# A GRU and a mixture of experts on one core: the state's dimensions dealt out anew, and the first loads reordered

## The chip, the cores and the metric

The kernel runs on one core of a Trainium2 chip. The metric is the device time of one execution in microseconds (us); for the kernel before it is 1520.65 us, the median of five runs (1519.76 to 1525.86).

## The reference

Sequences `x` of shape [8, 256, 512] go through a GRU whose start state is `cond_2048` [8, 512]; its outputs go through a mixture of eight experts (two for each token) and a shared feed-forward part, and the result is added to `x`:

```python
def cell(h, x):
    gi = x @ W_ih + b_ih
    gh = h @ W_hh + b_hh
    i_r, i_z, i_n = jnp.split(gi, 3, axis=-1)
    h_r, h_z, h_n = jnp.split(gh, 3, axis=-1)
    r = jax.nn.sigmoid(i_r + h_r)
    z = jax.nn.sigmoid(i_z + h_z)
    n = jnp.tanh(i_n + r * h_n)
    h_new = (1.0 - z) * n + z * h
...
combine = jnp.sum(topk_w[..., None] * jax.nn.one_hot(topk_ids, E, dtype=x.dtype), axis=1)
gu = jnp.einsum('th,ehf->etf', x, w_gate_up)
act = _silu_and_mul(gu)
eo = jnp.einsum('eti,eih->eth', act, w_down)
routed = jnp.einsum('te,eth->th', combine, eo)
shared = _silu_and_mul(x @ w_sh_gate_up) @ w_sh_down
```

W_ih and W_hh are [512, 1536] in float32, 3.15 MB each.

## The kernel before

Time is cut into 16 blocks of 16 steps; a block of all 8 sequences is 128 rows. The state has 512 dimensions on 128 partitions in NQ = 4 slots. Before the change, slot q of partition 32j+i holds dimension 128j+32q+i. With that order a 128x128 tile in which partition 32j+b holds sequence b's dimensions 128j to 128j+127 becomes, by VectorE's transpose of 32x32 squares, the transposed state. Weights whose rows are state dimensions have to be loaded in the same order: `by_state` (L122) gives four loads for it, each to 32 partitions.

**The weights' places.** w_ih, w_hh and later the experts' weights share one tile `we`: w_ih has the place of experts 6 and 7, w_hh that of experts 4 and 5. Biases and a row of ones have small places in `we` too.

**The head.** In program order: x_0 on SyncE's and ScalarE's queues in turn (8 loads, L119), the two bias rows on ScalarE's (L137, L138), w_ih in 12 loads on SyncE's (L142), h0 in 4 on ScalarE's (L147), x_1 in 8 and w_hh in 12 on SyncE's (L119, L152). VectorE turns x_0 (L299), and with that x_2's 8 loads are issued on SyncE's queue. Then, for each of the three gates g (r, z, n), `project(0, g)` (L340) multiplies x_0 with w_ih: four pieces, one for each q, of four matmuls to the four column groups; `spread_bias` (L256) spreads the bias row over 128 partitions by a matmul with ones, and ScalarE copies it to `bias` (L260). `end` (L355) adds product and bias into `gi` on VectorE. After gate 1 the sums for r and z are stored to DRAM (gid_rz, L366), after gate 2 those for n (gid_n, L368), both from SyncE's queue. `load_seeds` (L378) reads them back on SyncE's queue, four steps at a time, in the layout of the gates' banks: seeds (r and z) and seeds_n. `turn_seeds` (L388) transposes those for n. Then x_1 is transposed and the first gate of block 1 is projected (the loop at L862), the gates' banks are filled with the seeds (`open_gate`, L397, a ScalarE copy at L403), and step 0 begins.

Products, bias spreads and most other matmul results of the head share three PSUM buffers (tag "mm").

**A step** (`step`, L413) is 48 matmuls at L419, for each gate r, n, z 16: state slot q as the stationary operand (8 columns), w_hh's 128 columns of group j as the moving operand, the sum on top of the seeds in the gate's bank. VectorE transposes the bank (L430), ScalarE and VectorE make the gates and the new state (L438 to L455), GpSimd copies it to `hc` (L458). float32 matmuls are recorded twice, so a step has 96 records at L419.

**What fills PE between steps.** A queue of pieces, written out by the loop at L866, with a cost for each: the projections of later blocks, and from block 2 on the shared part (L705, L310). Blocks 0 and 1 take pieces of 33 times 0.86 each. Routing (`choose` at L472, and so on) has its own steps. Weights for the shared part and the experts are issued one entry of `loads` at a time on GpSimd's queue (L165), those of experts 4 and 5 after the last step. Last come 39 tiles of 128 routed rows, gathered (L752), transposed (L766), multiplied with their expert's weights (L659, L785) and added to the output by an indirect DMA (L791).

Of the kernel before, what the change touches and what calls it, by code (L numbers as in the profile page):

```python
# [13 lines left out]
ALU = mybir.AluOpType  # L14
# [11 lines left out]
def kernel(  # L26
# [100 lines left out]
    load_x(0, (nc.sync, nc.scalar))  # L127
# [10 lines left out]
    nc.scalar.dma_start(bias_h, b_hh[0 : 2 * D].unsqueeze(0))  # L138
    for g in range(3):
        cols = slice(g * D, (g + 1) * D)  # L140
        for ps, src in by_state(w_ih[:, cols]):
            nc.sync.dma_start(wih[ps, :, cols], src)  # L142
    h = state.tile([P, NQ, 32], F32, name="h")
    nc.vector.memset(h, 0.0)
    h0v = h0.rearrange("b (j q i) -> b j q i", q=NQ, j=4)
    for j in range(4):
        nc.scalar.dma_start(h[32 * j : 32 * j + B], h0v[:, j])  # L147
    load_x(1)
    for g in (0, 2, 1):
        cols = slice(g * D, (g + 1) * D)  # L150
        for ps, src in by_state(w_hh[:, cols]):
            nc.sync.dma_start(whh[ps, :, cols], src)  # L152
# [16 lines left out]
    def load_shared():  # L169
        load(*((wg[ps, :, 0:E], src) for ps, src in by_state(w_gate)))  # L170
        up = w_sh_gate_up.rearrange("d (two c f) -> two c d f", two=2, f=IM)
        down = w_sh_down.rearrange("(c f p) n -> c p f n", p=P, f=NF)
        for c in range(NSH):
            for two_i in range(2):
                parts = [(wsu[c][ps, :, two_i, :], src) for ps, src in by_state(up[two_i, c])]
                load(*parts[:2])
                load(*parts[2:])
            for f in range(NF):
                load((wsd[c][:, f, :], down[c][:, f, :]))

    def load_expert(e):
        for q in range(NQ):
            load((we[:, e, q, :], w_gate_up[e, q * P : (q + 1) * P, :]))
        for f in range(NF):
            load((we[:, e, NQ + f, :], w_down[e, f * P : (f + 1) * P, :]))


    ident = const.tile([P, P], F32, name="ident")
    make_identity(nc, ident)
# [4 lines left out]
    for st in [*seeds, seeds_n, seed_hn, *states]:  # L194
        nc.vector.memset(st, 0.0)

# [55 lines left out]
    nc.vector.tensor_tensor(bias_row[:, 0 : 2 * D], bias_row[:, 0 : 2 * D], bias_h, ALU.add)  # L252
    one = we[0:1, 2, 0, 0:P]
    nc.vector.memset(one, 1.0)
# [7 lines left out]
    b_hn = b_hh[2 * D : G3].rearrange("(j m) -> j m", j=4)  # L262
    for j in range(4):
        nc.gpsimd.dma_start(seed_hn[32 * j : 32 * j + B], b_hn[j].partition_broadcast(B))
# [32 lines left out]
    def transpose_x(k):  # L297
        xT = two.tile([P, NG, NQ, 32], F32, tag="xrT", name=f"xT_{k}")
        nc.vector.transpose(  # L299
            xT.rearrange("p g q s -> p (g q s)"), x_tiles.pop(k).rearrange("p g m -> p (g m)")  # L300
        )
        xT_of[k] = xT
        if k + 2 < NB:
            load_x(k + 2)
# [35 lines left out]
    def project(k, g):  # L340
# [13 lines left out]

        def end():  # L355
            nc.vector.tensor_tensor(
                gi[:, :, g, :],
                box["ps"].rearrange("p (j m) -> p j m", j=4),
                bias[:, g * D : (g + 1) * D].rearrange("p (j m) -> p j m", j=4),
                ALU.add,  # L360
            )
            if g > 0:
                to = gi_dram[k][g % 2].rearrange("j b t n -> (b t) j n")
                projected.add((k, "rzn"[g]))
                if g == 1:
                    nc.sync.dma_start(to.rearrange("p j (a n) -> p j a n", a=2), gi[:, :, 0:2, :])  # L366
                else:
                    nc.sync.dma_start(to, gi[:, :, 2, :])  # L368
# [9 lines left out]
    def load_seeds(c, of="nz"):  # L378

        k, o = divmod(c * SC, TS)  # L380
        steps = slice(o, o + SC)
        for g in of:
            assert (k, g) in projected
            tile_, src = (seeds_n, gi_dram[k][0]) if g == "n" else (seeds[c % NS], gi_dram[k][1])
            for j in range(4):
                nc.sync.dma_start(tile_[32 * j : 32 * j + B], src[j, :, steps, :])
# [18 lines left out]
    whh_v = whh.rearrange("p q (a j m) -> p q a j m", a=3, j=4)  # L405
# [5 lines left out]
    def step(n):  # L411
# [3 lines left out]
        for g, bank in banks.items():  # L415
            a = "rzn".index(g)
            for q in range(NQ):
                for j in range(4):
                    nc.tensor.matmul(  # L419
                        bank[32 * j : 32 * j + B, 0:P],  # L420
                        hT[:, q, 0:B],
                        whh_v[:, q, a, j, :],
                        start=False,
                        stop=(q == NQ - 1),
                        skip_group_check=True,
                    )
# [413 lines left out]
    transpose_x(0)  # L840
    nc.vector.transpose(states[0].rearrange("p q b -> p (q b)"), h.rearrange("p q i -> p (q i)"))
    for g in range(3):
        pieces = project(0, g)
        for piece in pieces[:-1]:
            piece[1]()
        spread_bias(g)
        pieces[-1][1]()
        if g > 0:
            load_seeds(0, "nzn"[g])
    turn_seeds(0)  # L850
    load_seeds(1)
# [3 lines left out]
    projections.append((0, lambda: transpose_x(1)))  # L855
# [6 lines left out]
    for _ in range(1 + NQ):  # L862
        projections.popleft()[1]()
    for g in banks:
# [128 lines left out]
```

## Time and profile before

| | |
|---|---|
| median of five runs | 1520.65 us |
| the profiled execution | 1519.18 us, its span 1517.4 |
| granted TensorE clock over the span | 0.989 |
| PE busy | 1443.5 us (95%) |
| VectorE, ScalarE, GpSimd busy | 49%, 28%, 17% |
| first matmul of step 0 | 55.95 us |
| w_ih's last load lands | 21.12 us |
| w_hh's last load lands | 39.51 us |
| matmuls L419, records | 24,576 of 273 ns |

The profile is of one execution, from the span's start. A group's mean is the time of one instruction from start to end; matmuls overlap, so the busy time of a group is less than count times mean. In the chain of work that ended last each row is a start, a length and what ran, and a DMA's length is from its issue to its landing. A DMA share of 1 means that the 16 DMA engines are full. In the view of waits a row names who waited for whom, the sum, the number of waits and the longest.

### The profile page before, as it was taken

How to read it: one execution, taken by the hardware profiler on the slowest of the kernel's cores; microseconds unless marked ns; L12 is line 12 of the kernel's file. 1: busy time of each engine (PE TensorE's matmuls, PEld its weight loads, DVE VectorE, ACT ScalarE, POOL GpSimd, SP SyncE). 2: the span in 40 equal slices, each digit the busy share in tenths (PEclk: the TensorE clock that was granted, in tenths of full speed). 3: DMA queues.
4: the chain of work that ended last, by engine and by line, in shares of the span. 5: the costliest groups of instructions: out<-in, count | busy, mean ns of one | idle time of the engine just before them, and what ended most of it. 6: DMA issues, size and time to landing. Idle time of an engine off the chain costs nothing.

```text
span 1517.4 us, 75290 instructions
## 1 busy us (share of the span) xinstructions
PE 1443.5 (95%) x33154; PEld 1057.7 (70%) x33154; DVE 750.8 (49%) x2782; ACT 423.2 (28%) x1786; POOL 258.6 (17%) x505
## 2 busy tenths in 40 slices
PE   4699999999999999999999999999999999999996
PEld 1487777787778787877787777887787754444442
DVE  2356455555565656565656565556565541222221
ACT  0122223323323333332333333333333311222221
POOL 1122311111110001010101010101011221444442
PEclk8799999999999999999999999999999999999998
DMA  8244623122211011111101120111011432555553
GB/s 184 83 109 119 94 56 70 49 63 70 63 50 41 18 45 34 29 49 28 47 18 39 28 56 14 35 28 42 15 48 42 97 90 84 95 86 96 85 96 49
DMA packets 70122, 92.78 MB, mean 61 GB/s; under 512 B 13538, under 2 KB 46370, under 8 KB 69796
## 3 DMA queue, kind: packets, MB, share of 16 engines
q0 software_dynamic: 16352, 39.67, 13.3%
q1 hardware_dynamic: 53056, 48.14, 12.5%
q8 instruction: 261, 4.28, 1.3%
q14 instruction: 65, 0.53, 0.1%
q10 hardware_dynamic: 388, 0.16, 0.0%
HBM read 56.55 MB, written 31.37 MB: 58 GB/s over the span
## 4 chain that ended last, share of the span: by engine, by line
PE 90%; DMA 3%; DVE 3%; issue 2%; ACT 1%; SPq 0%; POOLq 0%; DVEq 0%; ACTq 0%; POOL 0%
PE ps_r L419 16%; PE ps_n L419 15%; PE gu_s L705 15%; PE ps_z L419 14%; PE gu_t L659 9%; PE gip L310 9%; PE po L310 7%; PE yp L785 4%; DMA we<-in_L_cond_W_hh_dram 1%; DMA we<-in_L_cond_W_ih_dram 1%; DVE zT L430 1%; DVE hn L454 0%; ACT z L449 0%; DVE hT L455 0%; PE ps_z L766 0%
## 5 line engine op out<-in xcount | busy, mean ns | idle before, releaser
L419 PEld LDWEIGHTS ps_r<-we,hT 128*8 128x8 f32 x8192 | 226.5, 89 | 119.5 <-ACT ps_z L403 72.6
L419 PE MATMUL ps_r<-we,hT 128*8 128x128 f32 x8192 | 282.4, 273 | 18.5 <-DVE hT L455 10.3
L419 PE MATMUL ps_n<-we,hT 128*8 128x128 f32 x8192 | 288.9, 273 | 1.5 <-issue 0.9
L419 PE MATMUL ps_z<-we,hT 128*8 128x128 f32 x8192 | 285.9, 273 | 3.8 <-issue 3.7
L705 PE MATMUL gu_s<-hc,wsu 128*32 128x256 f32 x4096 | 251.1, 379 | 1.4 <-issue 1.3
L458 POOL COPY hc<-hT 128x32 f32<-128x32 f32 x256 | 62.7, 245 | 1057.5 <-DVE hT L455 1049.0
L419 PEld LDWEIGHTS ps_n<-we,hT 128*8 128x8 f32 x8192 | 234.4, 90 | 8.0 <-issue 7.0
L419 PEld LDWEIGHTS ps_z<-we,hT 128*8 128x8 f32 x8192 | 235.6, 90 | 5.0 <-issue 4.8
L310 PE MATMUL gip<-we,xT 128*32 128x512 f32 (+1 forms) x1976 | 197.6, 507 | 31.2 <-DVE xT L299 22.8
L705 PEld LDWEIGHTS gu_s<-hc,wsu 128*32 128x32 f32 x4096 | 151.3, 110 | 76.4 <-issue 14.9
L438 ACT ACTIVATE r<-rT 128x32 f32<-128x32 f32 x256 | 58.6, 229 | 520.7 <-DVE rT L430 516.0
L430 DVE STREAM_TRANSPOSE rT<-ps_r 128x128 f32<-128x128 f32 x256 | 80.5, 314 | 190.7 <-PE ps_r L419 190.2
L659 PE MATMUL gu_t<-we,xrT 128*128 x312 | 146.7, 593 | 0.2 <-ACT xrT L768 0.2
L430 DVE STREAM_TRANSPOSE nT<-ps_n 128x128 f32<-128x128 f32 x256 | 80.8, 316 | 123.5 <-PE ps_n L419 123.2
L310 PE MATMUL po<-wsd,act_s 128*32 128x256 f32 (+1 forms) x1408 | 138.2, 476 | 0.0
L310 PEld LDWEIGHTS gip<-we,xT 128*32 128x32 f32 x1976 | 73.6, 111 | 84.2 <-issue 73.3
L403 ACT COPY ps_n<-seed_hn 128x128 f32<-128x128 f32 x256 | 68.8, 269 | 85.2 <-DVE nT L430 82.4
L650 DVE TENSOR_TENSOR act_t<-gu_t,act_t 128x256 f32<-128x256 f32 x39 | 16.6, 425 | 146.5 <-ACT act_t L649 146.5
L430 DVE STREAM_TRANSPOSE zT<-ps_z 128x128 f32<-128x128 f32 x256 | 81.0, 317 | 12.8 <-PE ps_z L419 5.1
L791 POOL DMA_INDIRECT out_dram<-y,row x39 | 61.8, 1585 | 124.6 <-DVE y L788 111.5
L446 ACT ACTIVATE nn<-nt 128x32 f32<-128x32 f32 x256 | 58.8, 230 | 80.9 <-DVE nt L444 79.7
L659 PEld LDWEIGHTS gu_t<-we,xrT 128*128 128x128 f32 x312 | 53.3, 190 | 38.7 <-issue 38.0
(160 smaller groups left out, 1204.4 us busy)
## 6 DMA issues: line engine op xcount, KB each, us to landing
gid_rz<-gi SPq DMA_DIRECT2D x16, 512.0 KB
seeds<-gid_rz SPq DMA_DIRECT2D x256, 32.0 KB
we<-in_L_ffn_w_gate_up_dram POOLq DMA_DIRECT2D x32, 256.0 KB
gid_n<-gi SPq DMA_DIRECT2D x16, 256.0 KB
seeds_n<-gid_n SPq DMA_DIRECT2D x256, 16.0 KB
wsu<-_L_ffn_w_sh_gate_up_dram POOLq DMA_DIRECT2D x32, 128.0 KB
rows<-hr SPq DMA_DIRECT2D x128, 32.0 KB
we<-in_L_ffn_w_down_dram POOLq DMA_DIRECT2D x16, 256.0 KB
```

The costliest lines, as they stand in the source:

```text
L310: nc.tensor.matmul(ps[32 * c : 32 * c + 32], lhs(c), rhs, start=start, stop=stop, skip_group_check=True,)
L403: nc.scalar.copy(banks[g][:, 0:P], src[g])
L419: nc.tensor.matmul(bank[32 * j : 32 * j + B, 0:P], hT[:, q, 0:B], whh_v[:, q, a, j, :], start=False, stop=(q == NQ - 1), skip_group_check= ...
L430: nc.vector.transpose(gT.rearrange("p a b -> p (a b)"), banks[g][:, 0:P])
L438: nc.scalar.activation(r, gr, AF.Sigmoid)
L446: nc.scalar.activation(nn, nt, AF.Tanh)
L458: nc.gpsimd.tensor_copy(hc_of_block(k).rearrange("p g q (c t) -> p q g c t", t=TS)[:, :, :, :, t], new.rearrange("p q (g c) -> p q g c", c=2),
L650: nc.vector.tensor_tensor(act, ps[:, 0:IM], act, ALU.mult)
L659: nc.tensor.matmul(box["ps"], lhs(q), w_up(q), start=(q == 0), stop=(q == NQ - 1))
L705: nc.tensor.matmul(box["ps"][32 * g : 32 * g + 32, two_i, :], wsu[c][:, q, two_i, fs], hc_of[m][:, :, q, :], start=(two_i == 0 and q == 0) ...
L785: nc.tensor.matmul(box["y"], lhs, rhs, start=(f == 0), stop=(f == NF - 1))
L791: nc.gpsimd.indirect_dma_start(out=out.rearrange("b t d -> (b t) d"), out_offset=bass.IndirectOffsetOnAxis(ap=laid["row"][:, i : i + 1], a ...
```

## The change

Slot q of partition 32j+i now holds dimension 128q+32j+i, that is, 128q+p for partition p. Rows of w_hh, of the router's w_gate and of the shared part's weights then go to 128 partitions in plain order: w_hh in three loads (one for each gate), w_gate in one, the shared part's in 16 instead of 32. The experts' w_gate_up, multiplied with rows that were stored in the permuted order, now goes by `by_state` in four loads of 32 partitions, instead of four of 128. w_ih stays with `by_state` (x comes in by the same squares as before), its groups j = 0, 1 on SyncE's queue and j = 2, 3 on ScalarE's. The columns of a gate are dealt out in the same way, so `end` reads product and bias, and a step reads w_hh, in runs of 32 (four runs at a stride of 128).

In order of issue: the biases come ahead of x_0; w_hh follows w_ih on SyncE's queue, then x_2. ScalarE's queue gets h0 and x_1, then the bias copies, and for block 0 the stores gid_rz and gid_n and the reads of the first seeds. The first memsets are those that the head needs first, and the bias sum stands among them. The three bias spreads come ahead of the projections, x_1's transpose ahead of gate 2, and block 1's first gate ahead of `turn_seeds` and `load_seeds(1)`. x_3 is loaded with x_1's transpose.

```diff
         v = w.rearrange("(j q i) n -> j i q n", j=4, i=32)
         return [(slice(32 * j, 32 * j + 32), v[j]) for j in range(4)]
 
-    load_x(0, (nc.sync, nc.scalar))
 
 
     we = wts.tile([P, E, NW, D], F32, name="we")
...
     bias_h = we[0:1, 0, 3:5].rearrange("p w n -> p (w n)")
     nc.scalar.dma_start(bias_row, b_ih.unsqueeze(0))
     nc.scalar.dma_start(bias_h, b_hh[0 : 2 * D].unsqueeze(0))
+    load_x(0, (nc.sync, nc.scalar))
     for g in range(3):
         cols = slice(g * D, (g + 1) * D)
-        for ps, src in by_state(w_ih[:, cols]):
-            nc.sync.dma_start(wih[ps, :, cols], src)
+        for i, (ps, src) in enumerate(by_state(w_ih[:, cols])):
+            (nc.sync, nc.scalar)[i // 2].dma_start(wih[ps, :, cols], src)
+    w_hh_v = w_hh.rearrange("(q p) n -> p q n", p=P)
+    for g in (0, 2, 1):
+        cols = slice(g * D, (g + 1) * D)
+        nc.sync.dma_start(whh[:, :, cols], w_hh_v[:, :, cols])
+    load_x(2)
     h = state.tile([P, NQ, 32], F32, name="h")
     nc.vector.memset(h, 0.0)
-    h0v = h0.rearrange("b (j q i) -> b j q i", q=NQ, j=4)
-    for j in range(4):
-        nc.scalar.dma_start(h[32 * j : 32 * j + B], h0v[:, j])
-    load_x(1)
-    for g in (0, 2, 1):
-        cols = slice(g * D, (g + 1) * D)
-        for ps, src in by_state(w_hh[:, cols]):
-            nc.sync.dma_start(whh[ps, :, cols], src)
+    one = we[0:1, 2, 0, 0:P]
+    nc.vector.memset(one, 1.0)
     wg = wts.tile([P, NQ, 32], F32, name="wg")
     nc.vector.memset(wg, 0.0)
     wsu = [wts.tile([P, NQ, 2, IM], F32, name=f"wsu_{c}") for c in range(NSH)]
...
         loads.append(issue)
 
     def load_shared():
-        load(*((wg[ps, :, 0:E], src) for ps, src in by_state(w_gate)))
+        load((wg[:, :, 0:E], w_gate.rearrange("(q p) e -> p q e", p=P)))
         up = w_sh_gate_up.rearrange("d (two c f) -> two c d f", two=2, f=IM)
         down = w_sh_down.rearrange("(c f p) n -> c p f n", p=P, f=NF)
         for c in range(NSH):
             for two_i in range(2):
-                parts = [(wsu[c][ps, :, two_i, :], src) for ps, src in by_state(up[two_i, c])]
-                load(*parts[:2])
-                load(*parts[2:])
+                src = up[two_i, c].rearrange("(q p) f -> p q f", p=P)
+                for qs in (slice(0, NQ // 2), slice(NQ // 2, NQ)):
+                    load((wsu[c][:, qs, two_i, :], src[:, qs]))
             for f in range(NF):
                 load((wsd[c][:, f, :], down[c][:, f, :]))
 
     def load_expert(e):
-        for q in range(NQ):
-            load((we[:, e, q, :], w_gate_up[e, q * P : (q + 1) * P, :]))
+        for ps, src in by_state(w_gate_up[e]):
+            load((we[ps, e, 0:NQ, :], src))
         for f in range(NF):
             load((we[:, e, NQ + f, :], w_down[e, f * P : (f + 1) * P, :]))
 
 
-    ident = const.tile([P, P], F32, name="ident")
-    make_identity(nc, ident)
     seeds = [const.tile([P, SC, 2 * P], F32, name=f"seeds_{i}") for i in range(NS)]
     seeds_n = const.tile([P, SC, P], F32, name="seeds_n")
     seed_hn = const.tile([P, P], F32, name="seed_hn")
     states = [const.tile([P, NQ, 32], F32, name=f"hT_{i}") for i in range(NH)]
-    for st in [*seeds, seeds_n, seed_hn, *states]:
+    nc.vector.memset(seeds[0], 0.0)
+    nc.vector.memset(seed_hn, 0.0)
+    nc.vector.tensor_tensor(bias_row[:, 0 : 2 * D], bias_row[:, 0 : 2 * D], bias_h, ALU.add)
+    for st in [*seeds[1:], seeds_n, *states]:
         nc.vector.memset(st, 0.0)
+    ident = const.tile([P, P], F32, name="ident")
+    make_identity(nc, ident)
 
     tri = const.tile([P, P], BF16, name="tri")
     make_upper_triangular(nc, tri, val=1.0, diag=False)
...
         ]
         for i in range(NB)
     ]
-    nc.vector.tensor_tensor(bias_row[:, 0 : 2 * D], bias_row[:, 0 : 2 * D], bias_h, ALU.add)
-    one = we[0:1, 2, 0, 0:P]
-    nc.vector.memset(one, 1.0)
 
     def spread_bias(g):
         ps = ps_mm.tile([P, D], F32, tag="mm", name=f"biasp_{g}")
...
         nc.tensor.matmul(ps, one, bias_row[:, cols], start=True, stop=True)
         nc.scalar.copy(bias[:, cols], ps)
 
-    b_hn = b_hh[2 * D : G3].rearrange("(j m) -> j m", j=4)
+    b_hn = b_hh[2 * D : G3].rearrange("(q j i) -> j q i", q=NQ, j=4)
     for j in range(4):
-        nc.gpsimd.dma_start(seed_hn[32 * j : 32 * j + B], b_hn[j].partition_broadcast(B))
+        nc.gpsimd.dma_start(
+            seed_hn[32 * j : 32 * j + B].rearrange("b (q i) -> b q i", q=NQ),
+            b_hn[j].partition_broadcast(B),
+        )
 
 
     rows = dram.tile([B, T, D], F32, name="rows")
...
             xT.rearrange("p g q s -> p (g q s)"), x_tiles.pop(k).rearrange("p g m -> p (g m)")
         )
         xT_of[k] = xT
-        if k + 2 < NB:
+        if 0 < k < NB - 2:
             load_x(k + 2)
 
     def multiply(ps, lhs, rhs, start, stop):
...
                 stop=(q == NQ - 1 and cols.stop == D),
             )
 
+        def by_group(t_):
+            return t_.rearrange("p (q j i) -> p j q i", q=NQ, j=4)
+
         def end():
             nc.vector.tensor_tensor(
-                gi[:, :, g, :],
-                box["ps"].rearrange("p (j m) -> p j m", j=4),
-                bias[:, g * D : (g + 1) * D].rearrange("p (j m) -> p j m", j=4),
+                gi[:, :, g, :].rearrange("p j (q i) -> p j q i", q=NQ),
+                by_group(box["ps"]),
+                by_group(bias[:, g * D : (g + 1) * D]),
                 ALU.add,
             )
             if g > 0:
                 to = gi_dram[k][g % 2].rearrange("j b t n -> (b t) j n")
                 projected.add((k, "rzn"[g]))
+                by = nc.sync if k else nc.scalar
                 if g == 1:
-                    nc.sync.dma_start(to.rearrange("p j (a n) -> p j a n", a=2), gi[:, :, 0:2, :])
+                    by.dma_start(to.rearrange("p j (a n) -> p j a n", a=2), gi[:, :, 0:2, :])
                 else:
-                    nc.sync.dma_start(to, gi[:, :, 2, :])
+                    by.dma_start(to, gi[:, :, 2, :])
 
         return [
             matmul_piece(lambda cols, q=q: issue(q, cols), end if q == NQ - 1 else None)
...
             assert (k, g) in projected
             tile_, src = (seeds_n, gi_dram[k][0]) if g == "n" else (seeds[c % NS], gi_dram[k][1])
             for j in range(4):
-                nc.sync.dma_start(tile_[32 * j : 32 * j + B], src[j, :, steps, :])
+                by = nc.sync if c else nc.scalar
+                by.dma_start(tile_[32 * j : 32 * j + B], src[j, :, steps, :])
 
     def turn_seeds(c):
 
...
         src = {"r": seeds[c % NS][:, t, 0:P], "z": seeds[c % NS][:, t, P : 2 * P], "n": seed_hn}
         nc.scalar.copy(banks[g][:, 0:P], src[g])
 
-    whh_v = whh.rearrange("p q (a j m) -> p q a j m", a=3, j=4)
+    whh_v = whh.rearrange("p q (a k j i) -> p q a j k i", a=3, k=NQ, j=4)
     hc_of = {}
 
     def hc_of_block(k):
...
             for q in range(NQ):
                 for j in range(4):
                     nc.tensor.matmul(
-                        bank[32 * j : 32 * j + B, 0:P],
+                        bank[32 * j : 32 * j + B, 0:P].rearrange("b (k i) -> b k i", k=NQ),
                         hT[:, q, 0:B],
                         whh_v[:, q, a, j, :],
                         start=False,
...
 
 
     transpose_x(0)
+    h0v = h0.rearrange("b (q j i) -> b j q i", q=NQ, j=4)
+    for j in range(4):
+        nc.scalar.dma_start(h[32 * j : 32 * j + B], h0v[:, j])
+    load_x(1, (nc.scalar,))
+    for g in (2, 0, 1):
+        spread_bias(g)
     nc.vector.transpose(states[0].rearrange("p q b -> p (q b)"), h.rearrange("p q i -> p (q i)"))
     for g in range(3):
-        pieces = project(0, g)
-        for piece in pieces[:-1]:
+        if g == 2:
+            transpose_x(1)
+        for piece in project(0, g):
             piece[1]()
-        spread_bias(g)
-        pieces[-1][1]()
         if g > 0:
             load_seeds(0, "nzn"[g])
-    turn_seeds(0)
-    load_seeds(1)
     load_shared()
 
     projections = deque()
-    projections.append((0, lambda: transpose_x(1)))
     for k in range(1, NB):
         for g in range(3):
             projections.extend(project(k, g))
             if g == 1 and k + 1 < NB:
                 projections.append((0, lambda k=k: transpose_x(k + 1)))
 
-    for _ in range(1 + NQ):
+    for _ in range(NQ):
         projections.popleft()[1]()
+    turn_seeds(0)
+    load_seeds(1)
     for g in banks:
         open_gate(0, g)
     for k in range(NB):
```

## The prediction

> **What bounds the kernel now.** I read the page from the top, then the first 60 us. The slices (38 us each) and the shares of the chain that ended last:
>
> ```profile
> span 1517.4 us, 75290 instructions
> PE   4699999999999999999999999999999999999996
> DMA  8244623122211011111101120111011432555553
> PE 90%; DMA 3%; DVE 3%; issue 2%; ACT 1%; SPq 0%; POOLq 0%; DVEq 0%; ACTq 0%; POOL 0%
> ```
>
> PE is busy everywhere except in the first slice and a half, where the DMA row is at 8. So the body is PE's instruction stream, which the change hardly touches in number, and the question is the head. The chain in order of time shows how the head ends, up to the first matmul of step 0:
>
> ```profile
> 30.05 9.46 DMA we<-in_L_cond_W_hh_dram
> ...
> 39.53 0.31 SPq L119
> ...
> 39.95 2.85 DMA gid_rz<-gi
> ...
> 44.29 2.22 DMA gid_n<-gi
> ...
> 47.52 1.62 DMA seeds_n<-gid_n
> ...
> 49.89 0.68 DVE xT L299
> ...
> 50.71 5.24 PE gip L310 x32
> 55.95 0.87 PE ps_r L419 x32
> ```
>
> SyncE's queue is the culprit. The first block's rz projection is added by 24.2 us (timeline: the L356 add at 23.47 for 0.69), but its store gid_rz is issued at 39.95, because w_hh's loads and two blocks of x stand ahead of it on SyncE. After it come, in series, a store, four reads, a store, four reads, the turn of the seeds, x's transpose and block 1's first projection. The waits of SyncE's queue say why it is stuck so long:
>
> ```profile
> SPq L119 <- DMA we<-in_L_cond_W_hh_dram: 6.9, 8, 1.0
> SPq L142 <- DMA we<-in_L_cond_b_ih_dram: 3.2, 1, 3.2
> ```
>
> An x load waits for a w_hh load that it doesn't need. In the chain, w_hh's fourth load (issued 22.91) lands at 30.03 and frees its twelfth at 30.05: the queues hold eight loads in flight, and a ninth waits for one eight earlier, whichever engine issued it. The transfers' speed, by windows (last columns: clock, DMA share, GB/s):
>
> ```profile
> 9.00:19.00 10.00, 7.58 (x42) 1.87 (x46) 1.45 (x7) 0.59 (x1) 0.00 (x0) 1.00 1.06 212
> 24.00:38.00 14.00, 3.96 (x30) 0.84 (x22) 0.85 (x2) 0.59 (x1) 0.00 (x0) 0.72 1.06 211
> 1231.00:1233.00 2.00, 2.00 (x36) 0.94 (x32) 0.22 (x1) 0.38 (x1) 0.95 (x2) 1.00 0.98 356
> 1251.00:1253.00 2.00, 2.00 (x45) 1.17 (x37) 0.00 (x0) 0.00 (x0) 0.00 (x0) 1.00 0.97 393
> ```
>
> The first two are w_ih and w_hh, each load to 32 partitions: the DMA engines are full and move 212 GB/s. The last two are expert weights to 128 partitions, same 2 KB rows: full, too, at 375 on average.
>
> **The change, part by part.** Times below are of the profiled execution (1519.18 us, of which 1517.4 is the span); the median of the five runs is 1520.65, 1.5 above it. I work out when step 0 starts, 55.95 now.
>
> *w_ih by two queues, biases first.* The 3.2 us that SyncE waits for a bias go. By 5.0 us the one-microsecond windows moved 0.50 MB of the 3.41 MB of x_0 and w_ih. The remaining 2.91 MB take 13.7 us at 212 GB/s (end 18.7) or 7.8 at 375 (end 12.8). Each load still goes to 32 partitions; what two queues at once do is not in this trace. I take 212, the row with the same destination, and keep 375 as the other end. The Trainium skill, page SBUF — State Buffer, section on issuing two DMAs to hit both halves, speaks against this part: two concurrent loads to opposite halves gained it only 6%, which would make the end 17.9. No run here shows that yet.
>
> *w_hh to 128 partitions.* 3.15 MB in three loads: 8.4 us at 375 against 14.9 at 212. The expert rows have the same shape, so I take 375. It ends between 21.2 and 33.6, well before step 0 needs it, so its speed counts only through the eight in flight.
>
> *ScalarE's queue.* It now issues 2 biases, 4 loads of x_0, 6 of w_ih, 4 of h0 and 8 of x_1 before spread_bias's copies, and gid_rz, gid_n and eight seed reads after them. The first projection's PSUM tile needs a bias copy done (three "mm" buffers, three biasp tiles), so what holds ScalarE holds PE. x_1's last load waits for loads up to eight earlier: w_ih's last, and probably w_hh's first third, 1.05 MB or 2.8 us; then x_1's own first half, 2.0 us (x_0's load in the chain, 0.74 to 2.76). ScalarE is free at 18.7 + 2.8 + 2.0 = 23.5. The ends: 20.7 if no w_hh load is in the way, 29.1 if all are.
>
> *From there to step 0.* The table load (1.28) and one copy (0.59) and 0.1 of gaps: 25.5. Gates 0 and 1 of the projection without a pause: a cold gate 5.24 (the 50.71 row; PE was idle and the clock at 0.5), a warm one 32 records at 0.107 = 3.43: 34.2. The add, 0.69 and 0.2 of gaps: gid_rz goes out on ScalarE at 35.1 instead of 39.95. The same series follows, as ScalarE now waits for each store: to the end of the seeds_n issues is 47.85 - 39.95 = 7.9, then a bank copy 0.27, so L419 starts at 43.3. Sigmoid's table load (1.28) now stands behind the bank copies and costs some 0.3 on step 0. Sum 43.6. Gate 2, x_1's transpose and block 1's first projection (3.43 + 0.68 + 3.43, to about 41.1) now run under the seeds' round trip; the 6.8 us from 49.13 to 55.95 that stood behind it go. PE's pause, 41.1 to 43.3, is 2.2 us; the clock fell 2.3 us after 27.96, so I charge no cold start, and 1.7 if it falls (5.24 less 3.43). turn_seeds ends at 35.1 + 9.2 + 0.8 = 45.1, before L444 wants it (step 0 start + 2.7).
>
> Gain 55.95 - 43.6 = 12.3 us: 1506.9 in the profiled execution, 1508.3 by the median.
>
> *What costs nothing.* L419's moving operand becomes four runs of 32. The logits already read hc so:
>
> ```profile
> L472 PE MATMUL lgp<-hc,wg 128*32 128x128 f32 x128 | 6.9, 273 | 0.7 <-POOL hc L458 0.7
> L419 PE MATMUL ps_n<-we,hT 128*8 128x128 f32 x8192 | 288.9, 273 | 1.5 <-issue 0.9
> ```
>
> Both last 273 ns, and eight L472 records take 0.22 us (1160.42 to 1160.64), 27 each, like L419's 0.87 for 32. Zero, then; upper end under rival E. L356's add gets broken runs: L453 (runs of 8) and L444 (none) both take 192 ns, so zero, and it runs beside PE. Expert loads go to 32 partitions, 1.24 us each at 212 instead of 0.7: the last is issued by 1249.95 and the first tile's matmul starts at 1277.0, so 27 us cover them. wsu and wg need 19 fewer issues at 0.56 on GpSimd, which is idle 83% of the time. Whether the lighter traffic changes PE's "issue" pauses is open: after 56 us they sum to 7.3 us, so between 7 less and 7 more; I take none. SyncE keeps x_2, x_3 and load_seeds(1), wanted four steps on. The reordered memsets and make_identity fill idle time before 10 us.
>
> **The rivals** (times by the median).
>
> B, **two queues double w_ih's rate**: it ends at 12.8, everything moves 5.9 earlier: 1502.4; with no w_hh load ahead of x_1, 1499.6. For it: 375 GB/s is there for whoever reaches all partitions. Against: no row has 32-partition loads above 212 for long.
>
> C, **a wait takes the place of the one removed**: ScalarE's x_1 loads, and behind them the bias copies and PE, wait for all of w_hh: free at 29.1, 1513.9. For it: SyncE did just this behind w_hh. Against: 12 of ScalarE's small loads can be ahead of it.
>
> D, **hidden anyway**: the same, and w_hh stays at 212 (14.9 us): free at 35.6, step 0 at 55.7, 1520.4: no change. Against: the expert rows.
>
> E, **slower**: L419's broken reads. If each of the four runs cost one more column (27.2 / 128 = 0.21 ns), a matmul is 0.85 ns longer, 24,576 of them 20.9 us, less the 12.3: 1529.3. It decides from 0.5 ns each (no gain left), and from 0.69 is slower by more than 0.3%. For it: L472 never comes in runs of 32. Against: its 27 ns.
>
> **How the numbers follow.** 0.3%, 4.6 us, is about what can be told from no change. Forecast (1505 to 1511.5) 0.44; B 0.24; C 0.13; D 0.10; E 0.09. Predicted 1508. The range leaves out E and most of D and takes in B with some of the open pauses: 1498 to 1517. Faster: forecast, B and C, 0.81; same: D, 0.10; slower: E, 0.09.
>
> **What would show it.** gid_rz on ScalarE's queue near 35 and L419's first row near 43.5; ScalarE's wait before the first bias copy ending on an x_1 load near 25; windows of w_ih at 212 and of w_hh at 375; L419 still 273 ns and 0.87 per gate. Wrong if w_ih's window shows 300 or more (B), if the bias copy waits past w_hh's landing (C), or if steps get longer than 4.33 us (60.28 less 55.95) in the body (E).

## The result and the profile after

The changed kernel takes 1516.56 us (median of 31 runs, 1510.60 to 1523.24), the kernel before 1521.65 in the same comparison (56 runs): a ratio of 0.9965, 95% interval [0.9956, 0.9974], 5.1 us less. The profiled execution took 1514.91 us, 4.3 less than that of before. The gain is real, and by the medians less than half of the 12.3 us forecast (1508 us).

The top of the page after the change, the same rows as before (span; slices of PE and DMA, 38 us each; shares of the chain that ended last):

```profile
span 1513.1 us, 75235 instructions
PE   3999999999999999999999999999999999999996
DMA  7234522222211111110201120111011443555553
PE 90%; DVE 3%; DMA 3%; issue 2%; ACT 1%; ACTq 0%; POOLq 0%; DVEq 0%; SPq 0%; POOL 0%
```

PE's first slice went from 4 to 3 and its second from 6 to 9, since the work of the head lies elsewhere now; the body is as it was. So the difference is in the head again. Its chain in order of time (start, length, what):

```profile
10.48 8.68 DMA we<-in_L_cond_W_ih_dram
19.17 9.72 DMA we<-in_L_cond_W_hh_dram
...
28.91 1.78 DMA x<-in_x_dram
30.71 2.40 DMA x<-in_x_dram
33.11 9.12 PE gip L312 x64
...
43.05 2.81 DMA gid_rz<-gi
...
47.30 2.19 DMA gid_n<-gi
...
51.27 1.06 PE ps_r L426 x32
```

Step 0 starts at 51.27 instead of 55.95: 4.7 of the 5.1 us. The store gid_rz, which was to go out at 35.1, goes out at 43.05, later than before the change (39.95), because the sums themselves are late: PE begins the first projection at 33.11. The reason stands in the first rows of the chain. w_hh's third load goes out at 19.17, the moment a load of w_ih (issued 10.48) has landed; it lands at 28.89, and at 28.91 a load of x_1 goes out. That load has nothing to do with w_hh. Between 19.17 and 28.91 the two queues issue seven loads, three of x_1 on ScalarE's and four of x_2 on SyncE's; the eighth has to wait until w_hh's third load has landed. This is the limit of eight that the kernel before showed, now between ScalarE's queue and SyncE's. The trace's instruction records show where the eight come from: each issue names a semaphore (a counter) that its landing raises, and all the issues of SyncE and ScalarE take turns on eight of them. The x_1 load of 28.91 has the one (number 106) that w_hh's third load had at 19.17; GpSimd's issues have eight of their own (110 to 117). So the limit lies in the program's semaphores; whether the queues have a limit of their own, no run shows. w_hh's first two loads (landed at 22.16 and 24.79) had x_2's loads on SyncE behind them (22.18 and 24.80), so that of x_1's loads only the fourth met w_hh. All that stands behind the load on ScalarE waits too, by the view of waits for ScalarE (sum, number, longest):

```profile
ACT L259 <- DMA x<-in_x_dram: 31.2, 1, 31.2
```

and by ScalarE's own row of time, where the eight issues of x_1 last from 21.13 to 31.14 and the table load ahead of the bias copies follows:

```profile
21.13 10.01 ACTq L119 DMA_DIRECT2D x<-in_x_dram  x8
31.17 1.28 ACT L259 ACT_TABLE_LOAD   x1 [31.17 <-DMA x<-in_x_dram]
```

The rates, by windows (last column GB/s): w_ih by two queues, and then w_hh alone to 128 partitions:

```profile
9.00:10.00 1.00, 0.47 (x1) 0.00 (x0) 0.02 (x1) 0.00 (x0) 0.00 (x0) 1.00 1.09 217
12.00:13.00 1.00, 0.00 (x0) 0.00 (x0) 0.00 (x0) 0.00 (x0) 0.00 (x0) 1.00 1.06 229
...
21.00:22.00 1.00, 0.00 (x0) 0.00 (x0) 0.00 (x0) 0.00 (x0) 0.00 (x0) 1.00 1.09 372
24.00:25.00 1.00, 0.00 (x0) 0.00 (x0) 0.00 (x0) 0.00 (x0) 0.00 (x0) 1.00 1.06 390
```

The layout of 128q+32j+i does for w_hh what the expert rows promised (375): the windows from 21 to 25 us average 369. Two queues do little for w_ih: the five windows from 9 to 14 us average 219 GB/s (205 to 229), against 212 of one queue. From 5 us on they did more: 5 to 14 us averages 233, against 210 in the run below with w_ih on one queue.

The step's matmuls with their broken reads, from the groups:

```profile
L426 PE MATMUL ps_n<-we,hT 128*8 128x128 f32 x8192 | 287.2, 273 | 0.4
```

273 ns, as before the change, and 32 records in the middle of a step still take 0.87 us: reading w_hh in four runs of 32 costs nothing.

### The profile page after: what moved, and what is told of

Read it like the earlier page. It is cut to its first block, busy times and chain, and to the rows that moved or that the text cites. A ratio compares the mean times of both kernels' runs of the same rounds, so it can differ in the third digit from the quotient of the medians.

```text
span 1513.1 us, 75235 instructions
## 1 busy us (share of the span) xinstructions
PE 1444.1 (95%) x33154; PEld 1058.2 (70%) x33154; DVE 750.2 (50%) x2782; ACT 422.3 (28%) x1786; POOL 250.9 (17%) x486
## 4 chain that ended last, share of the span: by engine, by line
PE 90%; DVE 3%; DMA 3%; issue 2%; ACT 1%; ACTq 0%; POOLq 0%; DVEq 0%; SPq 0%; POOL 0%
PE ps_r L426 16%; PE ps_n L426 15%; PE gu_s L712 15%; PE ps_z L426 14%; PE gip L312 9%; PE gu_t L666 9%; PE po L312 7%; PE yp L792 4%; DMA we<-in_L_cond_W_ih_dram 1%; DMA we<-in_L_cond_W_hh_dram 1%; DVE zT L437 1%; DVE hn L461 0%; DVE hT L462 0%; ACT z L456 0%; DMA x<-in_x_dram 0%
## 5 line engine op out<-in xcount | busy, mean ns | idle before, releaser
L312 PE MATMUL gip<-we,xT 128*32 128x512 f32 (+1 forms) x1976 | 193.9, 502 | 24.3 <-DMA x<-in_x_dram 23.6
L312 PEld LDWEIGHTS gip<-we,xT 128*32 128x32 f32 x1976 | 70.2, 111 | 79.9 <-issue 42.5
```

The source lines that it names most:

```text
L312: nc.tensor.matmul(ps[32 * c : 32 * c + 32], lhs(c), rhs, start=start, stop=stop, skip_group_check=True,)
```

## The experiments

Theory 1, after the comparison: the loads of SyncE's and ScalarE's queues share eight places in flight, and x_1's loads on ScalarE's queue met w_hh's last third in them, with the bias copies and PE behind. Rivals: what counts is the order in ScalarE's stream alone, the rate of the loads, or the end of w_hh's last load, whoever waits for what. The runs came in three groups, each against the kernel before on its own chip (medians 1508.65, 1507.85 and 1518.82 us), so they are compared by their ratio to it. With "sums" I mean the addition of product and bias for gates r and z, and "a third" is one of w_hh's three loads.

**x_1 off ScalarE's queue.**

```diff
-    load_x(1, (nc.scalar,))
+    load_x(1, (nc.gpsimd,))
```

> The changed kernel with one edit: x_1's eight loads go out on GpSimd's queue, not on ScalarE's. Theory 1 (slots): ScalarE was held to 31.2 us because x_1's fourth load stood behind w_hh's third, eight loads earlier; without x_1 it is free after h0's last load, near 18, and PE's first projection starts near 20 instead of 33.1. gid_rz then meets the next slot, that of an x_2 load that SyncE issues only when w_hh is in, and goes out near 31 instead of 43.05; step 0 near 39.5 instead of 51.3, and the time 12 us below the changed kernel's 1516.6: 1504 to 1505. Theory 2 (bytes): the first projection waits for w_ih's and w_hh's 6.3 MB whichever queue x_1 is on; then PE still starts near 31 to 33 and the time stays within 2 us of 1516.6.

1491.5 us, ratio 0.9881 [0.9858, 0.9904], 17 us below the kernel before by the medians. ScalarE is free at 18.84 instead of 31.17, and the store follows the sums (made at 30.48) at once. The 31 us that I had expected of it came out by luck: I had it wait for a load of x_2, and it waited for the sums. ScalarE's issues, and the last rows of the chain before step 0:

```profile
30.54 0.40 ACTq L372 DMA_DIRECT2D gid_rz<-gi  x1
33.61 1.39 ACTq L393 DMA_DIRECT2D seeds<-gid_rz  x4
35.10 0.39 ACTq L374 DMA_DIRECT2D gid_n<-gi  x1
```

```profile
35.10 2.31 DMA gid_n<-gi
...
39.18 1.06 PE ps_r L426 x32
```

Step 0 starts at 39.18, 12.1 us before that of the changed kernel, by an edit that moves eight loads of 32 KB. So the loads of x_1 on ScalarE's queue were what ate the gain. That they did it through the shared eight, and not just by standing in the stream, is for the next runs.

**x_1 stays, the bias copies go ahead of it.**

```diff
+    for g in (2, 0, 1):
+        spread_bias(g)
...
     for j in range(4):
         nc.scalar.dma_start(h[32 * j : 32 * j + B], h0v[:, j])
     load_x(1, (nc.scalar,))
-    for g in (2, 0, 1):
-        spread_bias(g)
```

> The changed kernel with one edit: the three bias spreads, and so ScalarE's three bias copies, stand ahead of h0's and x_1's loads in ScalarE's order. Theory 1 (slots): the copies run after ScalarE's last w_ih load is issued (12.6), PE starts when a whole gate of w_ih is in, near 15 to 17; ScalarE is still held by x_1 to 31.2, and gid_rz goes out then instead of at 43.05: step 0 near 39.4, the time near 1504.7. Theory 2 (bytes): PE starts near 31 to 33 all the same, and the time stays within 2 us of 1516.6.

1495.28 us, ratio 0.9917 [0.9886, 0.9947]. The sums are made at 26.18, but the store stands behind x_1's issues, which still wait for w_hh's last third:

```profile
14.81 14.03 DMA we<-in_L_cond_W_hh_dram
...
31.69 1.81 DMA x<-in_x_dram
...
34.55 6.45 PE gip L312 x32
41.00 0.87 PE ps_r L426 x32
```

That third lands at 28.84, x_1's last load goes out at 31.69, the store at 32.14, as the theory has it. Step 0 came at 41.00, not at the time expected: x_1 is now late as well, and block 1's first projection runs just before step 0 at a low clock (granted 0.50 from 34 to 38 us), 6.45 us instead of 3.43.

**w_hh back to 32 partitions.**

```diff
-        nc.sync.dma_start(whh[:, :, cols], w_hh_v[:, :, cols])
+        for j in range(4):
+            ps = slice(32 * j, 32 * j + 32)
+            nc.sync.dma_start(whh[ps, :, cols], w_hh_v[ps, :, cols])
```

> The changed kernel with w_hh in twelve loads to 32 partitions each instead of three to 128; the order of the state's dimensions stays new. If the partitions set the rate, w_hh moves near 212 GB/s instead of 369, its last load lands 3 to 6 us later (32 to 35 instead of 28.9), ScalarE is free as much later, and the time is 1519 to 1522. If the rate comes from the size of a load or from the queue, w_hh lands near 29 as before and the time stays at 1516 to 1517.

1508.27 us, ratio 0.9985 [0.9968, 1.0002]: nothing that can be told from the kernel before. The windows from 21 to 25 and 25 to 29 us move 212 and 208 GB/s, where the changed kernel moved 369 from 21 to 25 and had w_hh in at 28.89. Here its last load lands at 32.95, and x_1 comes in that much later:

```profile
24.12 9.64 DMA x<-in_x_dram
...
35.74 1.71 DMA x<-in_x_dram
37.45 9.06 PE gip L314 x64
...
55.64 1.06 PE ps_r L428 x32
```

Step 0 is at 55.64, where it was before the change (55.95). So the whole net gain of the change hangs on w_hh's loads to 128 partitions: with them the wait on ScalarE is 4.3 us shorter (31.2 against 35.5). The same edit took the loads from three to twelve; what the windows show of it is the rate.

**w_ih back to one queue.**

```diff
-            (nc.sync, nc.scalar)[i // 2].dma_start(wih[ps, :, cols], src)
+            nc.sync.dma_start(wih[ps, :, cols], src)
```

> The changed kernel with all twelve w_ih loads on SyncE's queue instead of half on ScalarE's. If two queues bring w_ih little (219 GB/s between 10 and 14 us against 212 in the kernel before), w_ih ends at 19 to 21 us, w_hh's last load lands near 28, ScalarE is released by the same load as now, and the time stays within 2 us of 1516.6. Rival (two queues reach both halves and are worth much): w_ih ends 4 us later or more and the time is over 1520.

1505.40 us, ratio 0.9973 [0.9959, 0.9988], which overlaps that of the changed kernel. The window from 9 to 14 us moves 211 GB/s. w_ih is in at 20.8, no later than from two queues (21.1), and w_hh at 30.2 instead of 28.9 (I had expected 28). ScalarE's issues of x_1 now begin earlier and end no earlier:

```profile
17.04 15.39 ACTq L119 DMA_DIRECT2D x<-in_x_dram  x8
32.46 1.28 ACT L259 ACT_TABLE_LOAD   x1 [32.46 <-DMA x<-in_x_dram]
```

They take 15.4 us with no load of w_ih or w_hh on ScalarE's own queue. So it is SyncE's loads that hold ScalarE's: the order within one stream cannot do that. Step 0 shows something else. PE paused 2.27 us ahead of it, no longer than in the changed kernel (2.22), yet here the clock fell (granted 0.62 from 53 to 55 us) and the first gate is slow, 1.75 us instead of 1.06:

```profile
53.28 1.75 PE ps_r L426 x32
```

**The kernel before, its store on ScalarE's queue, and on GpSimd's.** These two take nothing of the change but the route of block 0's stores and first seed reads (the second has `nc.gpsimd` in place of `nc.scalar`):

```diff
+                by = nc.sync if k else nc.scalar
...
-                    nc.sync.dma_start(to.rearrange("p j (a n) -> p j a n", a=2), gi[:, :, 0:2, :])
+                    by.dma_start(to.rearrange("p j (a n) -> p j a n", a=2), gi[:, :, 0:2, :])
...
-                    nc.sync.dma_start(to, gi[:, :, 2, :])
+                    by.dma_start(to, gi[:, :, 2, :])
...
-                nc.sync.dma_start(tile_[32 * j : 32 * j + B], src[j, :, steps, :])
+                by = nc.sync if c else nc.scalar
+                by.dma_start(tile_[32 * j : 32 * j + B], src[j, :, steps, :])
```

> The kernel before, with block 0's stores and the first seed reads on ScalarE's queue. Theory 1 (the two queues share the wait for the eighth issue before): part or all of the gain of the run on GpSimd's queue is lost, for the store waits for a load of x_1, x_2 or w_hh that SyncE issued; it goes out clearly later than 24.2 us, and the ratio lies between 0.993 and 1.0. Rival (only the order within one queue holds): it goes out near 24.2 as on GpSimd's queue, step 0 near 44, a ratio of 0.992.

1497.43 us, ratio 0.9936 [0.9913, 0.9959]. The store was not held: it met places that had long been free and went out at 23.56. The price of the shared eight fell on the other queue. SyncE's waits, and the chain:

```profile
SPq L119 <- DMA seeds<-gid_rz: 7.0, 1, 7.0
```

```profile
23.56 2.82 DMA gid_rz<-gi
...
38.03 9.27 DMA we<-in_L_cond_W_hh_dram
...
47.44 1.06 PE ps_z L421 x32
```

An x load on SyncE waits 7.0 us for a read of the seeds that ScalarE issued, and holds w_hh back until 29.35 (21.49 in the kernel before). So what I expected of the store fails (it and step 0 came as the rival had them), while the sharing shows in the opposite direction. Step 0 begins at 44.03, and its z gate waits for w_hh until 47.44.

> The kernel before, with nothing of the change but the route: block 0's stores of gid and the first reads of the seeds go out on GpSimd's queue instead of SyncE's. If the waiting in SyncE's queue, and not the loads' rate, is what held step 0: the store goes out right behind the additions, near 24.2 us, the last read lands near 37.5, step 0 starts near 44 instead of 55.95, 11 to 12 us below the kernel before, a ratio of 0.992: more than the whole change brought. If the rate of w_hh's loads decides: step 0 stays within 2 us of 55.95, a ratio of 0.999 or more.

1501.69 us, ratio 0.9963 [0.9946, 0.9980], as much as the whole change brought. The store goes out at 24.09, as expected; the rest does not follow:

```profile
24.09 9.86 DMA gid_rz<-gi
...
36.56 6.39 DMA gid_n<-gi
...
48.19 6.41 PE gip L310 x32
54.60 0.87 PE ps_r L421 x32
```

GpSimd's queue doesn't wait for the eight, but its store is on the same DMA engines behind w_hh's loads that SyncE has issued, and takes 9.86 us instead of 2.82. I had priced a store with the row of one that has the engines to itself. The Trainium skill (DMA: Bandwidth & Descriptors, section on issuing engines that are not separate DMA queues) says that transfers of all engines run on the same 16 DMA engines, and that issuing from several saves only the issuing time, usually small. The 9.86 us agree with the first half; the second is too little for this kernel, where moving x_1's eight issues brought step 0 forward by 12.1 us while each of them takes only 0.3 to 0.4 us to issue. Step 0 is only 1.4 us earlier than before the change, which is what the other expectation (the rate of w_hh's loads decides) said of it. The total gained more than that (by the interval 3.0 to 8.1 us), and where the rest came from I did not settle.

**x_1 and x_2 on GpSimd's queue, bias copies first.**

```diff
-    load_x(2)
...
+    for g in (2, 0, 1):
+        spread_bias(g)
...
-    load_x(1, (nc.scalar,))
-    for g in (2, 0, 1):
-        spread_bias(g)
+    load_x(1, (nc.gpsimd,))
+    load_x(2, (nc.gpsimd,))
```

> The changed kernel with the loads of x_1 and x_2 both on GpSimd's queue, and block 0's sixteen bias copies ahead of h0's loads in ScalarE's order. Theory 1 (a DMA issue of SyncE or ScalarE waits for the landing of the eighth issue before it on the two queues together): no load then stands between w_hh's three thirds and h0's four loads, so the store of gates r and z meets the first third (landed at 22.9 in the run with x_1 alone on GpSimd's queue), and goes out near 25 us; the two later reads meet the second and third thirds, which land by 28 to 29. Step 0 starts at 33.5 to 34.5 us instead of 39.2 with x_1 alone moved and 51.3 in the changed kernel: 17 us below the changed kernel, a ratio to the kernel before of 0.985. Rival (what is left in front of step 0 is w_hh's last third itself, whoever issues what): the store stays at 28 to 31 us and step 0 near 39, a ratio of 0.988.

1495.03 us, ratio 0.9909 [0.9884, 0.9934], not better than x_1 alone. The sums are made at 28.29; the store goes out at 32.69:

```profile
25.08 7.53 DMA x<-in_x_dram
...
32.69 3.11 DMA gid_rz<-gi
...
41.20 1.90 PE ps_r L425 x32
```

I had counted wrongly which load it meets: not w_hh's first third but a load of x_3, issued by SyncE when that third had landed (25.07), which then waited on the engines behind the other two and landed at 32.61. And the last third itself lands at 32.41, not at 28.87 as with x_1 alone moved: here sixteen loads of x are issued beside w_hh's.

**h0 there as well.** As the run before, and

```diff
-        nc.scalar.dma_start(h[32 * j : 32 * j + B], h0v[:, j])
+        nc.gpsimd.dma_start(h[32 * j : 32 * j + B], h0v[:, j])
```

> As the run before it (x_1 and x_2 on GpSimd's queue, bias copies ahead), with h0's four loads on GpSimd's queue too. Theory 1: the store of gates r and z then meets a load of w_ih, which has landed by 21, so ScalarE is never held ahead of it and the store waits for the projection alone; step 0 0 to 2 us earlier than in the run before it, a ratio of 0.984 to 0.985. Rival (w_hh's last third sets the end): no difference to the run before it, step 0 near 39.

1492.05 us, ratio 0.9900 [0.9877, 0.9923], the same as the run before. The sums are now made at 24.67, and the store still goes out at 32.94, for an x_3 load again: SyncE issued it at 14.51, directly behind w_hh's last third, and it lands at 32.86. Theory 1's number (out by the sums) fell with the same miscount; the rival's, no difference and step 0 near 39, was nearer (41.28).

**x_3 there as well, h0 on ScalarE.** The run with x_1 and x_2, and

```diff
-            load_x(k + 2)
+            load_x(k + 2, (nc.gpsimd if k == 1 else nc.sync,))
```

> The run with x_1 and x_2 on GpSimd's queue, with x_3's loads there too (there an x_3 load, issued by SyncE at 25.07 and landed at 32.61, held the store of gates r and z, whose sums were ready at 28.3, until 32.69). If only the eighth issue before it holds the store, it now meets w_hh's first third and goes out at 25 to 28.5, as soon as the sums are made. If the transfers are served in the order of their issue, it still lands behind w_hh's bytes, at 32 to 34, as in the run of the store on GpSimd's queue (9.86 us for it): step 0 then 40 to 41.5, 0 to 1 us before the run with x_1 and x_2. If a store passes the loads issued before it, it lands 3 us after its issue and step 0 starts at 36 to 37.

1500.35 us, ratio 0.9881 [0.9853, 0.9909]. No load of x is left in the store's way, and it goes out with the sums:

```profile
28.20 0.69 DVE gi L360
28.91 6.01 DMA gid_rz<-gi
...
40.41 1.90 PE ps_r L425 x32
```

Nothing was edited but the queue of x_3's loads, and the wait of 4.4 us in front of the store went to 0.02: the store was held by the landing of another queue's load. And the gain at step 0 is 0.8 us, because the store now spends 6.01 us instead of 3.11 behind w_hh's bytes. Both halves were expected; the landing at 34.92 is a microsecond later than the range. That the store stood behind w_hh's bytes, and did not move slowly among them, shows in the trace's packets: none of its 1 KB packets ends before 31 us, and 323 of its 512 KB move in the one microsecond from 32, when w_hh's 2 KB packets are nearly through. So for the end of the head the rival came nearer in these three runs: whether the issue waits or the bytes do, the store lands behind w_hh's last load (32.4 to 33.6 us).

**w_hh behind the store.** To have nothing heavy ahead of the store in either sense: the changed kernel with x_1 on GpSimd's queue and w_hh's three loads on ScalarE's, directly after gid_rz.

```diff
-    for g in (0, 2, 1):
-        cols = slice(g * D, (g + 1) * D)
-        nc.sync.dma_start(whh[:, :, cols], w_hh_v[:, :, cols])
...
-    load_x(1, (nc.scalar,))
+    load_x(1, (nc.gpsimd,))
...
+        if g == 1:
+            for g_ in (0, 2, 1):
+                cols = slice(g_ * D, (g_ + 1) * D)
+                nc.scalar.dma_start(whh[:, :, cols], w_hh_v[:, :, cols])
         if g > 0:
             load_seeds(0, "nzn"[g])
```

> The changed kernel with x_1's loads on GpSimd's queue and w_hh's three loads on ScalarE's queue directly behind block 0's store of gates r and z. Nothing heavy then stands ahead of the store, neither in the eight slots nor in the order of the bytes. The copies of the biases still stand behind h0's loads, so the sums are made near 29 to 30 as with x_1 alone moved, or earlier, near 25, if h0 was held by w_hh's bytes there; the store lands 3 us after its issue; w_hh's 8.5 us lie in front of the seeds' reads, so that it all lands 9 to 10 us behind the store's issue. Step 0 at 36 (sums at 25) to 40.5 (sums at 29.5); in the first case 3 us below the run with x_1 alone on GpSimd's queue, a ratio to the kernel before of 0.986; in the second no difference to it.

1512.59 us, ratio 0.9959 [0.9942, 0.9976]: back at the changed kernel's, and outside what I expected (step 0 at 36 to 40.5).

```profile
23.23 9.39 PE gip L309 x64
...
33.44 3.26 DMA gid_rz<-gi
...
38.10 9.16 DMA gid_n<-gi
...
49.04 1.90 PE ps_r L423 x32
```

The sums are late (33.40), since the bias copies stood behind h0's loads until 21.3; the store lands in 3.26 us as it should; then w_hh's bytes delay the second store, 9.16 us instead of 2.31, and the reads of it come after that, not beside it. I had counted one delay of 9 to 10 us behind the store where the series after it took 15.6. Of the two places tried, w_hh was cheaper ahead of the sums (step 0 at 39.18), where PE still has the first projection to do.

All runs in one table (us; "sums" is the end of the addition for r and z, "landed" the store's):

| kernel | sums | store out | landed | step 0 | ratio |
|---|---|---|---|---|---|
| before | 24.16 | 39.95 | 42.80 | 55.95 | 1 |
| changed | 43.03 | 43.05 | 45.86 | 51.27 | 0.9965 |
| x_1 on GpSimd's queue | 30.48 | 30.54 | 33.60 | 39.18 | 0.9881 |
| bias copies first | 26.18 | 32.14 | 35.29 | 41.00 | 0.9917 |
| w_hh to 32 partitions | 47.30 | 47.32 | 50.13 | 55.64 | 0.9985 |
| w_ih by one queue | 44.99 | 45.02 | 47.83 | 53.28 | 0.9973 |
| x_1, x_2 on GpSimd's | 28.29 | 32.69 | 35.80 | 41.20 | 0.9909 |
| and h0 | 24.67 | 32.94 | 35.83 | 41.28 | 0.9900 |
| x_1, x_2, x_3 on GpSimd's | 28.89 | 28.91 | 34.92 | 40.41 | 0.9881 |
| w_hh behind the store | 33.40 | 33.44 | 36.70 | 49.04 | 0.9959 |
| before, store on ScalarE's | 23.54 | 23.56 | 26.38 | 44.03 | 0.9936 |
| before, store on GpSimd's | 23.81 | 24.09 | 33.95 | 54.60 | 0.9963 |

The start of step 0 accounts for the difference to the kernel before within 2.6 us in every row but the last (4.2). The intervals of the ratios are 0.002 to 0.003 to either side, so the four rows between 0.988 and 0.991 can't be told apart by their times.

## Why the prediction was wrong

The direction held, the size did not. Step by step:

- *What bounds the kernel now.* Right: 4.7 of the 5.1 us are step 0's.
- *w_ih by two queues, biases first.* The rate from 9 us on was right (205 to 229 GB/s by windows against 212 taken), the end was not: w_ih's last load lands at 21.11, not 18.7, the same time as before the change (21.12). SyncE's wait for a bias is gone, but its w_ih loads wait 3.5 us for x_0's loads instead, and w_hh's first load, issued at 9.5 while w_ih was still coming in, takes a share of the engines. I had w_hh begin when w_ih ends. Rival B is out: only the one microsecond from 8 us shows over 300 GB/s (325). The Trainium skill (SBUF — State Buffer, section on issuing two DMAs to hit both halves) gives 6% for two concurrent loads; the runs here are to either side of it, 4% from 9 to 14 us (219 against 211 from one queue) and 11% from 5 to 14 (233 against 210).
- *w_hh to 128 partitions.* Right: 346 to 390 GB/s from 21 to 25 us, 369 on average, against 375; landed at 28.89 against 27.1, later by the term above.
- *ScalarE's queue.* **This step failed.** It had ScalarE free at 18.7 + 2.8 + 2.0 = 23.5; it was free at 31.17. Term by term: w_ih's end 2.4 later; "probably w_hh's first third", 2.8, was all three, 28.89 - 21.11 = 7.8, 5.0 more; x_1's rest 2.3 instead of 2.0. That is 7.7 us, and the whole miss at step 0 (51.27 - 43.6). The mechanism was on record as rival C, with 0.13; it had ScalarE free at 29.1. The argument against it, that 12 of ScalarE's small loads can be ahead, was a wrong count: what an issue waits for is the eighth issue before it on the two queues together, and with x_2's loads issued in between that was w_hh's last third for x_1's fourth load, however small the loads around it are. The sharing itself was in my own reading of the profile before ("whichever engine issued it"; that holds for SyncE and ScalarE, not for GpSimd).
- *From there to step 0.* Right in sum: 20.1 us forecast (43.6 - 23.5), 51.27 - 31.17 = 20.1 measured. The two projections took 9.12 instead of 8.67, the series behind the store 8.2 instead of 8.5, in which the 0.3 for sigmoid's table load was no cost: the first sigmoid waits for the transposed bank (0.28 us) after that load. The pause of PE before step 0 was 2.2 us, as forecast, and its first gate ran at full clock (1.06 us), but the reason I gave for that does not stand. In the kernel before, the clock fell 2.1 us after 27.96 (the window from 30 to 31 us shows 0.55), not 2.3, so a pause of 2.2 was no safe one; with w_ih by one queue a pause of 2.27 lowered the clock. The full clock was luck.
- *What costs nothing.* Right for the reads of w_hh (273 ns, 0.87 us for 32), so rival E is out. The rest of that list no run took apart.
- *Rival D*, no change, is what the run with w_hh to 32 partitions shows: ratio 0.9985, step 0 at 55.64.

## What to carry to other kernels

When a transfer is moved to another engine's queue, find out which semaphores the issues share, and count the issues over the queues together, in order: a row of small loads waits for a big one as soon as it is the eighth before one of them, and the engine's own work waits behind the row. Then ask what bytes are already on the DMA engines: an issue that is no longer held lands behind them all the same. Here the change with x_1's small loads on a third queue, off the engine that the path needs, took 1.19% off the time, and without that 0.35%.

## What the runs showed of the hardware

- The limit of eight, by the semaphores of this program, holds for SyncE's and ScalarE's queues together, in both directions (ScalarE's issues of x_1 took 10.0 to 15.4 us behind SyncE's w_hh; SyncE waited 7.0 us behind ScalarE's seed read). Loads on GpSimd's queue were not part of it: moving x_3's there ended a wait of 4.4 us.
- The same store of 512 KB took 2.82 us with free engines, 6.01 and 9.86 behind w_hh's loads, the last on a queue of its own.
- The length of PE's pause alone did not decide whether its clock fell. Pauses of 2.22 us (changed kernel), 2.32 (w_hh to 32 partitions) and 2.67 (x_1 moved) before step 0 left its first gate at 1.06 us. One of 2.27 (w_ih by one queue) brought it to 1.75, and one of 2.10 us in the head of the run with x_1, x_2 and x_3 moved, from 27.54 to 29.64, was followed by a granted clock of 0.57 from 30 to 34 us. What else decides it no run was made to show. In the traces' records of the granted clock every stretch between two changes is a whole multiple of 3.41 us (3.41, 6.83, 10.24, 13.65, 17.07 and 23.89 in the head), as if the clock were set anew on a beat of that length; then it would matter where on the beat a pause falls. That is inferred, not tested. The four pauses of 5.4 to 10.6 us before step 0 (x_1 and x_2 moved, with h0 or x_3 too, and w_hh behind the store) all brought the first gate to 1.90. The windows of the run with x_1 and x_2 (clock in the last column but two) show the granted clock at about half, then back:

```profile
41.00:46.00 5.00, 4.79 (x96) 3.62 (x100) 1.73 (x5) 2.67 (x8) 0.00 (x0) 0.53 0.14 40
46.00:51.00 5.00, 5.00 (x128) 3.24 (x124) 2.17 (x10) 1.34 (x7) 1.34 (x3) 1.00 0.13 40
```

The three gates of step 0 take 5.0 us there (1.90, 1.71 and 1.39) instead of 2.8. With the store's landing, 1.3 to 2.2 us later, that is where the runs with x_2 moved as well lose what their sums, made 1.6 to 5.8 us earlier, had gained on the run with x_1 alone.
